# A fused cellular-automaton and convolution kernel: input rows asked for earlier, split rows of 256 columns, VectorE in program order

## The chip, the cores and the metric

The kernel runs on one core of a Trainium2 chip. A core has a matrix engine (TensorE, "PE"; its weight loads are "PEld"), a vector engine (VectorE, "DVE"), an activation engine (ScalarE, "ACT"), a general engine (GpSimd, "POOL") and a queue engine (SyncE, "SP") that here only issues DMAs. The engines run side by side and wait for each other through semaphores. Sixteen DMA engines carry all transfers. The metric is the time on the device in microseconds; lower is better.

## The reference

The input x has 32 images of 8 channels of 256 x 256 float32. Two layers follow each other, each on a group-normalised input. Layer 0, with the constants put in:

```python
drive = grid = x                       # x is normalised here, [32, 8, 256, 256]
for _ in range(15):                    # the lattice
    mapped = 3.9 * grid * (1.0 - grid)
    local = conv(mapped, K_local, groups=8)          # 3x3, each channel by itself
    physics = 0.7 * mapped + 0.3 * local
    grid = 0.85 * physics + 0.15 * drive
cml = clip(grid, 0.0001, 0.9999)
h = relu(conv(x, Wp, bp))              # NCA: 3x3, 8 -> 128 channels
nca = sigmoid(conv(h, Wu, bu))         # 1x1, 128 -> 8
gin = concatenate([x, cml, nca])       # 24 channels
g = sigmoid(conv(relu(conv(gin, Wg1, bg1)), Wg2, bg2))   # the gate: 3x3, then 1x1
out0 = g * cml + (1.0 - g) * nca
```

`out0` is added to the raw input. Layer 1 normalises the sum, quantises it to whole numbers between -127 and 127 with one scale for the whole batch, convolves it 3x3 from 8 to 8 channels, scales back, adds a bias and adds its own input.

## The kernel before

The program has two phases. Phase one computes layer 0, phase two layer 1. Phase two can start only when the largest value of all images is known.

Phase one works on eight groups of four images, and four kinds of work run in it at once:

- **Normalising** (`normalise`, L293 to L387). A pair of channels of one image is loaded into `xr`. VectorE takes statistics (L314, L315). TensorE averages them over the partitions (L322, L355) and VectorE finishes mean and deviation (L323 to L327, L357). GpSimd takes the power -1/2 of the variance (L358, `rstd_x`). VectorE then scales `xr` (L361). The result is written to memory twice. ScalarE copies it into `xq`, four column phases apart, for lattice and gate (`gs_s`). For NCA it is split in two float32 numbers of fewer digits, `hi` by a VectorE cast (L372) and `lo`, the rest, by a GpSimd subtraction (L373), which go to `xp_s` (L342). A row of `xp_s` has `PW` = 258 columns, of which the first and the last are zero, and so have the rows of the tiles `hi` and `lo`.
- **The lattice** (`lattice`, L392 to L557). One unit is one channel of four images, held in two sets `s` = 0, 1. A step of one set is a "half" (`half`, L480). Its matmuls (L499) fill two PSUM units `pt`. After each of three blocks of them a very small matmul `mark` follows (L274). VectorE empties the units into `gt` (L510) and computes the next state from `gt` (L520), each in two pieces. The state swaps between two layouts, `m_a` and `m_b`. After a half that writes `m_b`, GpSimd masks an edge (L525). After a half that writes `m_a`, SP issues two DMAs that exchange rows between tiles (`exchange`, L474 and L475), and the next step of this set needs them. 15 steps of two sets in 64 units are 1920 halves. The sources of the next unit (`d_a`, `d_b`, L462) and the stores of the last one also go out on SP, four after each half.
- **NCA** (`nca`, L576 to L644). An image is done in eight tiles of 32 rows. The input tile `im` of a tile has four DMAs (`rows`, L561 to L573). A unit (`hidden`, L579) is twelve matmuls (L585) into one PSUM unit, which ScalarE empties into `h` (L593). Eight units make a tile. After every two of them a drain of four matmuls (L601) follows, into `acc`. The tiles of `im` come from a pool with two buffers.
- **The gate** (`gate`, L705 to L836), one group behind. A tile has 120 matmuls (L759) over three sources `gin`, each of which takes two DMAs (`stage`, L656, L663). The same function also issues the two DMAs of `mix` (L672), which holds the values to be mixed. The rest of a tile is a list of "chores": mixing (`gate` and `y` on VectorE, L723 and L724), arranging (`f` on ScalarE, `d` and `f` on GpSimd, L685 to L689), staging the next tile, statistics (`st_y`, L730) and extremes with the store (`mx`, `mn`, L733 to L735).

These four are Python generators. `together` (L844) runs the lattice as the main one. After each half it takes one chore from the list, and then lets the others advance in proportion to fixed weights. The order in which the program states its instructions comes from this.

TensorE keeps this order as it stands. For the four other engines a scheduler decides the order, with the program's order as a priority:

```python
one.enter_context(tc.manual_schedule(engines={mybir.EngineType.PE}))
```

All PSUM units of lattice, NCA, gate and averages come from one pool `ps_u` with three buffers, so a unit can be written only when the one three places earlier has been emptied. All DMAs of phase one that the change touches are issued by SP, one after the other. An SP instruction that waits holds up those behind it.

NCA asks for the rows of the next tile after the sixth of the eight units, before the third drain:

```python
if i == 2:
    if done:
        nc.sync.dma_start(*done)
        done = None
    if t < NT8 - 1:
        ahead = rows(b, t + 1)
    elif all((b + 1, g) in ready for g in range(4)):
        loaded[b + 1] = rows(b + 1, 0)
```

Of the kernel before, what the change touches and what calls it, by code (L numbers as in the profile page):

```python
# [40 lines left out]
P = 128  # L41
# [11 lines left out]
PROWS = 268  # L53
ROW = 2 * C * PW
PART = PROWS * C * W
# [54 lines left out]
def kernel(  # L110
# [50 lines left out]

    xp_s = [dp.tile([PROWS, 2, C, PW], F32, name=f"xp_s{i}") for i in range(NBUF)]
    gs_s = [dp.tile([3, PROWS, C, W], F32, name=f"gs_s{i}") for i in range(NBUF)]
    y_s = [dp.tile([PROWS, C, W], F32, name=f"y_s{b}") for b in range(B)]

    with tc.tile_pool(name="prep", bufs=1) as pp, tc.tile_pool(name="prep2", bufs=2) as pp2:
# [23 lines left out]
        for t, at, n, w, rows in (  # L190
            *((t, 0, 2 * C, PW, ((0, 1), (257, 1))) for t in xp_s),
            *((t, j * PART, C, W, ((0, 1), (257, 1))) for t in gs_s for j in range(3)),
            *((t, 0, C, W, ((0, 1), (257, 5), (262, 5), (267, 1))) for t in y_s),
        ):
            k = 64 if w == W else 43
            for row, m in rows:
                borders.append(
                    (
                        dram_ap(t, at + row * n * w, [[w, m * n], [k, w // k], [1, k]]),
                        zt[: m * n, :k].unsqueeze(1).to_broadcast([m * n, w // k, k]),  # L200
                    )
                )
# [52 lines left out]
    with ExitStack() as one:  # L255


        one.enter_context(tc.manual_schedule(engines={mybir.EngineType.PE}))

# [3 lines left out]
        hp, xp, sp2, gp, gip = pool("hp", 4), pool("xp", 3), pool("sp2", 1), pool("gp", 3), pool("gip", 2)  # L263
        st, imp, wk, np_ = pool("st", 2), pool("imp", 2), pool("wk", 2), pool("np", 1)
        ps_u, ps_a, ps_m = pool("ps_u", 3, space=PSUM), pool("ps_a", 1, space=PSUM), pool("ps_m", 1, space=PSUM)
# [10 lines left out]
        fixed = lambda shape, name, dt=F32: np_.tile(shape, dt, name=name)  # L276
        hi, lo = fixed([P, 2, 2, PW], "hi", F32R), fixed([P, 2, 2, PW], "lo", F32R)
        for t in (hi, lo):
            for w in (0, PW - 1):
                G.memset(t[:, :, :, w].bitcast(F32), 0.0)  # L280
# [12 lines left out]
        def normalise(jobs):  # L293
# [36 lines left out]
            def stores(b, g, xq):  # L330
# [9 lines left out]
                for h in range(2):  # L340
                    for j, src in enumerate((hi, lo)):
                        nc.sync.dma_start(  # L342
                            dram_ap(
                                xp_s[b % NBUF],
                                (1 + P * h) * ROW + (C * j + 2 * g) * PW,
                                [[ROW, P], [PW, 2], [1, PW]],
                            ),
# [4 lines left out]
            def end(b, gs, xrs, e):  # L352
# [6 lines left out]
                for g, xr in zip(gs, xrs):  # L359
# [10 lines left out]
                    )  # L370
                    inner = lambda t: t[:, :, :, 1 : 1 + W]
                    V.tensor_copy(inner(hi), xr)  # L372
                    G.tensor_tensor(inner(lo), xr, inner(hi).bitcast(F32), ALU.subtract)  # L373
                    yield 0.05
# [186 lines left out]
        def rows(b, t):  # L561

            im = imp.tile([P, 2, 8, PW], F32R, name="im", tag="im")
            for k in range(2):
                for q in range(2):
                    nc.sync.dma_start(
                        im.bitcast(F32)[64 * q : 64 * q + 48, k],
                        dram_ap(
                            xp_s[b % NBUF], (32 * t + 16 * k + 8 * q) * ROW, [[PW, 48], [ROW, 8], [1, PW]]
                        ),  # L570
                    )
            return im
# [3 lines left out]
        def nca(b):  # L576
# [45 lines left out]
            for t in range(NT8):  # L622
                im = ahead
                acc = ps_a.tile([P, 512], F32, name="acc", tag="acc")
                for i in range(4):
                    hs = {}
                    for n in (i, i + 4):
                        hs[n], hs[n + 8] = hidden([im[64 * q : 64 * q + 48, :, n, :] for q in range(2)])
                        yield 1.4
                    if i == 2:  # L630
                        if done:
                            nc.sync.dma_start(*done)
                            done = None
                        if t < NT8 - 1:
                            ahead = rows(b, t + 1)
                        elif all((b + 1, g) in ready for g in range(4)):
                            loaded[b + 1] = rows(b + 1, 0)
                    if pend:
# [16 lines left out]

        def stage(b, t):  # L656

            src = gs_s[b % NBUF]
            gin = []
            for j in range(3):  # L660
                t_ = gip.tile([P, 4, W], F32, name=f"gin{j}", tag=f"gin{j}")
                for h in range(2):
# [5 lines left out]
                    )  # L668
                gin.append(t_)
            mix = gip.tile([P, 3, 2, W], F32, name="mix", tag="mix", bufs=1)  # L670
            for k in range(2):
# [3 lines left out]
                )  # L675
            return gin, mix

# [16 lines left out]
        def begin_gate(b):  # L694
            return scales(b), stage(b, 0)

# [8 lines left out]
        def gate(b):  # L705
# [39 lines left out]
            for t in range(NT8 + 1):  # L745
# [32 lines left out]

                def stage_(now):
                    if now["t"] < NT8 - 1:  # L780
                        now["ahead"] = stage(b, now["t"] + 1)
                    elif (b + 1) % GB:
                        staged[b + 1] = begin_gate(b + 1)

# [5 lines left out]

                steps = []
                if last:
                    steps.append(mix_)
                if t < NT8:
                    steps += [arrange_, stage_]
                if last:
# [280 lines left out]
```

## Time and profile before

Three runs took 13316.33 us in the median. The profile is of one execution.

| | |
|---|---|
| median of 3 runs (lowest to highest) | 13316.33 us (13310.97 to 13325.59) |
| profiled execution, its own time | 13288.75 us |
| profiled execution, span from first to last instruction | 13287.0 us |
| mean granted TensorE clock | 0.913 of full speed |
| DMA packets | 2486569, 1769.32 MB |
| DMA queue of SP | 58.7% of sixteen engines' span |
| start until NCA's first matmul | 206.6 us |
| phase one with lattice | until about 12340 us |
| last group's gate alone | until about 12720 us |
| phase two | the rest |

How to read it. A line of waits names the engine and the tile that waited, the one that ended the wait, the sum in microseconds, how often, and the longest. A wait with "issue" was ended by nothing that the profile shows. In a timeline a row gives start, duration, engine, line and operation, what is written from what, how many instructions were merged, and in brackets the idle time of the engine just before it. Each program matmul of four-byte numbers can stand as several records. PEclk is the clock that TensorE was granted; a digit of 9 means 0.9 to 1.0.

### The profile page before, as it was taken

Reading aid. Unit: us, or ns where it says so; the run is one execution under the profiler, and the core shown is the slowest. Engines: PE = TensorE matmul, PEld = TensorE weight load, DVE = VectorE, ACT = ScalarE, POOL = GpSimd, SP = SyncE. Lnnn points to the kernel's source line nnn. Section 1 sums busy time; section 2 is a strip of 40 time slices with the busy share of each in tenths; the row PEclk is TensorE's granted clock in tenths of the full one; section 3 lists DMA queues with packets and bytes.
Section 4 is the critical chain, followed back from the end, with each engine's and each line's share of the span. In section 5 each row is a group of like instructions: output and inputs, shape, how many; then the busy total and the mean of one; then the engine's idle time right before and its main releaser. Section 6 shows DMA issues by size and latency. Waiting matters only on the chain. (4 is left out here: it accounts for less than half of the span.)

```text
span 13287.0 us, 372338 instructions
## 1 busy us (share of the span) xinstructions
PE 11179.9 (84%) x165152; PEld 6938.4 (52%) x165152; DVE 7782.5 (59%) x11376; ACT 3789.6 (29%) x4034; POOL 1552.4 (12%) x2242
## 2 busy tenths in 40 slices
PE   4888888888888888888888888888888989889754
PEld 2555555555555555555555555555555555555532
DVE  4555555555555565555555556555655655556477
ACT  2222222222222222222222222222222222222233
POOL 1000011111111111111111111111111110001200
PEclk7999999999999999999999999999999999999877
DMA  6554566565666656665665666656666565555778
GB/s 164 94 102 95 102 134 129 123 132 127 135 127 130 134 128 126 130 136 122 132 132 123 134 135 130 127 127 132 128 132 133 127 127 116 113 109 123 179 242 257
DMA packets 2486569, 1769.32 MB, mean 133 GB/s; under 512 B 1034336, under 2 KB 2456032, under 8 KB 2484832
## 3 DMA queue, kind: packets, MB, share of 16 engines
q1 hardware_dynamic: 2392416, 1655.96, 58.7%
q10 hardware_dynamic: 92544, 89.54, 2.2%
q8 instruction: 1299, 21.28, 0.7%
q14 instruction: 310, 2.54, 0.1%
HBM read 1133.84 MB, written 474.94 MB: 121 GB/s over the span
## 5 line engine op out<-in xcount | busy, mean ns | idle before, releaser
L593 ACT ACTIVATE h<-pt,bp_sb 128x1024 f32<-128x1024 f32 x2048 | 2273.9, 1112 | 5982.6 <-PE pt L585 5978.3
L585 PE MATMUL pt<-im,wp_hi 48*128 48x512 f32 x12288 | 2869.3, 440 | 942.8 <-DMA im<-xp_s 769.3
L510 DVE SCALAR_TENSOR_TENSOR gt<-pt,d_b 128x650 f32<-128x650 f32 (+1 forms) x1920 | 1463.8, 763 | 2432.7 <-PE mark L274 1389.4
L499 PE MATMUL pt<-m_a,lw 64*64 64x325 f32 (+1 forms) x30720 | 2464.9, 439 | 354.9 <-DMA m_a<-m_a 223.6
L585 PE MATMUL pt<-im,wp_lo 48*128 48x512 f32 x12288 | 2660.7, 410 | 0.0
L510 DVE SCALAR_TENSOR_TENSOR gt<-pt,d_a 128x640 f32<-128x640 f32 (+1 forms) x1920 | 1446.8, 754 | 2013.6 <-PE mark L274 1059.9
L585 PEld LDWEIGHTS pt<-im,wp_hi 48*128 48x128 f32 x12288 | 1340.5, 194 | 2096.5 <-issue 1460.1
L499 PE MATMUL pt<-m_b,lw 64*64 64x256 f32 (+1 forms) x30720 | 2360.9, 425 | 67.6 <-DVE gt L510 38.1
L499 PEld LDWEIGHTS pt<-m_a,lw 64*64 64x64 f32 x30720 | 1462.2, 140 | 1185.8 <-issue 455.8
L499 PEld LDWEIGHTS pt<-m_b,lw 64*64 64x64 f32 x30720 | 1413.5, 136 | 881.8 <-issue 457.2
L759 PE MATMUL pt<-gin,gw 48*32 48x192 f32 (+2 forms) x61440 | 1321.0, 305 | 240.4 <-issue 228.7
L759 PEld LDWEIGHTS pt<-gin,gw 48*32 48x32 f32 x61440 | 1150.2, 109 | 588.8 <-issue 367.9
L585 PEld LDWEIGHTS pt<-im,wp_lo 48*128 48x128 f32 x12288 | 1345.7, 195 | 208.0
L520 DVE SCALAR_TENSOR_TENSOR m_a<-gt 128x640 f32<-128x640 f32 (+1 forms) x1792 | 1414.3, 789 | 58.5
L520 DVE SCALAR_TENSOR_TENSOR m_b<-gt 128x650 f32<-128x650 f32 (+1 forms) x1792 | 1385.7, 774 | 103.0 <-DVE gt L510 3.7
L525 POOL TENSOR_TENSOR m_b<-m_b,junk 128x36 f32<-128x36 f32 x896 | 241.9, 270 | 8498.1 <-DVE m_b L520 5232.4
L601 PE MATMUL acc<-h,wu_z 128*32 128x512 f32 x8192 | 1106.6, 611 | 0.0
L274 PE MATMUL mark<-qw 64*64 64x1 bf16 x5760 | 953.0, 165 | 3.2 <-issue 1.9
L687 POOL TENSOR_TENSOR d<-mix 128x256 f32<-128x256 f32 x512 | 554.7, 1101 | 1580.5 <-DVE gate L723 1146.5
L274 PEld LDWEIGHTS <-qw 64*64 64x64 bf16 x5760 | 642.8, 112 | 142.1 <-issue 10.3
L986 PE MATMUL pt<-qt,qw 128*128 128x512 bf16 (+1 forms) x864 | 235.0, 434 | 238.4 <-ACT ob L991 238.4
L685 ACT ACTIVATE f<-mix,sc 128x512 f32<-128x512 f32 x256 | 208.5, 815 | 679.5 <-DVE y L724 476.4
(109 smaller groups left out, 5445.8 us busy)
## 6 DMA issues: line engine op xcount, KB each, us to landing
im<-xp_s SPq DMA_DIRECT2D x1024, 387.0 KB
gin<-gs_s SPq DMA_DIRECT2D x1536, 192.0 KB
mix<-gs_s SPq DMA_DIRECT2D x512, 384.0 KB
d_a<-gs_s SPq DMA_DIRECT2D x2048, 36.0 KB
yb<-y_s ACTq DMA_DIRECT2D x28, 2432.0 KB
xp_s<-hi SPq DMA_DIRECT2D x256, 258.0 KB
xp_s<-lo SPq DMA_DIRECT2D x256, 258.0 KB
xr<-in_x_dram SPq DMA_DIRECT2D x128, 512.0 KB
```

The costliest lines, as they stand in the source:

```text
L274: T.matmul(one_[HIGH], qw[HIGH, 0, HIGH], qw[HIGH, 0, 0:1], start=True, stop=True)
L499: T.matmul(pt[dst], lw[src, c, w, dst], rhs[src], start=first, stop=not first)
L510: V.scalar_tensor_tensor(gt.rearrange("p (u c) -> p u c", u=2), pt[:, :, : w * n], FLOOR, d[:, ts, :].rearrange("p (u t) j -> p u (t j)", ...
L520: V.scalar_tensor_tensor(to, gt, 1.0, gt, ALU.subtract, ALU.mult)
L525: G.tensor_tensor(edge, edge, junk.unsqueeze(1).to_broadcast([P, TU, 2]), ALU.mult)
L585: T.matmul(ph[:, i, :].rearrange("p (h w) -> p h w", w=W), w[64 * i : 64 * i + 48, dx, :], rhs[:, :, dx : dx + W], start=(dx == 0 and w is ...
L593: S.activation(h.rearrange("p i c -> p (i c)"), ph.rearrange("p i c -> p (i c)"), AF.Relu, bias=bp_sb)
L601: T.matmul(acc[32 * g : 32 * g + 32], wu_z[:, 24 - 8 * i : 56 - 8 * i], hs[4 * g + i], start=(i == 0), stop=(i == 3),)
L685: S.activation(f, flat(mix[:, 0]), AF.Identity, bias=sc[:, 0:1], scale=sc[:, 2:3])
L687: G.tensor_tensor(d[:, cols], mix[:, 1, k], mix[:, 2, k], ALU.subtract)
L759: T.matmul(pa[32 * i : 32 * i + 32, h, to], gw[64 * h : 64 * h + 48, j, dx, :], gin[j][64 * h : 64 * h + 48, i, of], start=(j == 0 and n = ...
L986: T.matmul(pt[:, i:j, :], w[:, dx, :], qt[b % 2][h][:, k0 + i : k0 + j, dx : dx + W], start=(dx == 0), stop=(dx == 2),)
```

## The change

It has four parts.

1. NCA's `rows` of the next tile are issued after the first unit of a tile (`n == 0`), not after the sixth. The store of the tile before stays where it was.
2. `xp_s` has rows of 256 columns. `hi` and `lo` lose their two border columns. `im` is no longer taken from a pool: two fixed tiles `ims`, of which the border columns are zeroed once, take turns, and the DMAs write between the borders. A DMA's rows are now 1024 bytes where they were 1032.
3. `stage` is cut in two. `inputs` loads the three `gin` and becomes the first chore of a gate tile. `blend` loads `mix` and stays where `stage` was.
4. VectorE, too, keeps the program's order in phase one.

```diff
-ROW = 2 * C * PW
+ROW = 2 * C * W
...
-    xp_s = [dp.tile([PROWS, 2, C, PW], F32, name=f"xp_s{i}") for i in range(NBUF)]
+    xp_s = [dp.tile([PROWS, 2, C, W], F32, name=f"xp_s{i}") for i in range(NBUF)]
...
-            k = 64 if w == W else 43
+            k = 64
...
-        one.enter_context(tc.manual_schedule(engines={mybir.EngineType.PE}))
+        one.enter_context(tc.manual_schedule(engines={mybir.EngineType.PE, mybir.EngineType.DVE}))
...
-        hi, lo = fixed([P, 2, 2, PW], "hi", F32R), fixed([P, 2, 2, PW], "lo", F32R)
-        for t in (hi, lo):
+        hi, lo = fixed([P, 2, 2, W], "hi", F32R), fixed([P, 2, 2, W], "lo", F32R)
+        ims = [fixed([P, 2, 8, PW], f"im{i}", F32R) for i in range(2)]
+        for t in ims:
             for w in (0, PW - 1):
                 G.memset(t[:, :, :, w].bitcast(F32), 0.0)
...
-                                (1 + P * h) * ROW + (C * j + 2 * g) * PW,
-                                [[ROW, P], [PW, 2], [1, PW]],
+                                (1 + P * h) * ROW + (C * j + 2 * g) * W,
+                                [[ROW, P], [W, 2], [1, W]],
...
-                    inner = lambda t: t[:, :, :, 1 : 1 + W]
-                    V.tensor_copy(inner(hi), xr)
-                    G.tensor_tensor(inner(lo), xr, inner(hi).bitcast(F32), ALU.subtract)
+                    V.tensor_copy(hi, xr)
+                    G.tensor_tensor(lo, xr, hi.bitcast(F32), ALU.subtract)
...
-            im = imp.tile([P, 2, 8, PW], F32R, name="im", tag="im")
+            im = ims[(NT8 * b + t) % 2]
             for k in range(2):
                 for q in range(2):
                     nc.sync.dma_start(
-                        im.bitcast(F32)[64 * q : 64 * q + 48, k],
+                        im.bitcast(F32)[64 * q : 64 * q + 48, k, :, 1 : 1 + W],
                         dram_ap(
-                            xp_s[b % NBUF], (32 * t + 16 * k + 8 * q) * ROW, [[PW, 48], [ROW, 8], [1, PW]]
+                            xp_s[b % NBUF], (32 * t + 16 * k + 8 * q) * ROW, [[W, 48], [ROW, 8], [1, W]]
                         ),
...
                         hs[n], hs[n + 8] = hidden([im[64 * q : 64 * q + 48, :, n, :] for q in range(2)])
+                        if n == 0:
+                            if t < NT8 - 1:
+                                ahead = rows(b, t + 1)
+                            elif all((b + 1, g) in ready for g in range(4)):
+                                loaded[b + 1] = rows(b + 1, 0)
                         yield 1.4
-                    if i == 2:
-                        if done:
-                            nc.sync.dma_start(*done)
-                            done = None
-                        if t < NT8 - 1:
-                            ahead = rows(b, t + 1)
-                        elif all((b + 1, g) in ready for g in range(4)):
-                            loaded[b + 1] = rows(b + 1, 0)
+                    if i == 2 and done:
+                        nc.sync.dma_start(*done)
+                        done = None
...
-        def stage(b, t):
+        def inputs(b, t):
...
+            return gin
+
+        def blend(b, t):
+
+            src = gs_s[b % NBUF]
             mix = gip.tile([P, 3, 2, W], F32, name="mix", tag="mix", bufs=1)
...
-            return gin, mix
+            return mix
...
-                def stage_(now):
+                def inputs_(now):
                     if now["t"] < NT8 - 1:
-                        now["ahead"] = stage(b, now["t"] + 1)
+                        now["ahead"] = [inputs(b, now["t"] + 1)]
                     elif (b + 1) % GB:
-                        staged[b + 1] = begin_gate(b + 1)
+                        staged[b + 1] = [inputs(b + 1, 0)]
+
+                def blend_(now):
+                    if now["t"] < NT8 - 1:
+                        now["ahead"].append(blend(b, now["t"] + 1))
+                    elif (b + 1) % GB:
+                        staged[b + 1] = scales(b + 1), (*staged[b + 1], blend(b + 1, 0))
...
                 steps = []
+                if t < NT8:
+                    steps.append(inputs_)
                 if last:
                     steps.append(mix_)
                 if t < NT8:
-                    steps += [arrange_, stage_]
+                    steps += [arrange_, blend_]
...
-                while t < NT8 - 1 and "ahead" not in now and chores:
+                while t < NT8 - 1 and len(now.get("ahead", ())) < 2 and chores:
                     chores.pop(0)()
```

More of the change, by code (lines that the diff above doesn't have):

```diff
@@ L190 @@
         for t, at, n, w, rows in (
-            *((t, 0, 2 * C, PW, ((0, 1), (257, 1))) for t in xp_s),
+            *((t, 0, 2 * C, W, ((0, 1), (257, 1))) for t in xp_s),
             *((t, j * PART, C, W, ((0, 1), (257, 1))) for t in gs_s for j in range(3)),
@@ L263 @@
         hp, xp, sp2, gp, gip = pool("hp", 4), pool("xp", 3), pool("sp2", 1), pool("gp", 3), pool("gip", 2)
-        st, imp, wk, np_ = pool("st", 2), pool("imp", 2), pool("wk", 2), pool("np", 1)
+        st, wk, np_ = pool("st", 2), pool("wk", 2), pool("np", 1)
         ps_u, ps_a, ps_m = pool("ps_u", 3, space=PSUM), pool("ps_a", 1, space=PSUM), pool("ps_m", 1, space=PSUM)
@@ L694, in begin_gate @@
         def begin_gate(b):
-            return scales(b), stage(b, 0)
+            return scales(b), (inputs(b, 0), blend(b, 0))
         PARTS = (
```

## The prediction

> **What bounds the kernel now.** I read the page first, then the waits of TensorE and VectorE, the busy times by stage, and last the order of time around one wait.
>
> ```profile
> PE 11179.9 (84%) x165152; PEld 6938.4 (52%) x165152; DVE 7782.5 (59%) x11376; ACT 3789.6 (29%) x4034; POOL 1552.4 (12%) x2242
> ...
> PEclk7999999999999999999999999999999999999877
> DMA  6554566565666656665665666656666565555778
> ```
>
> TensorE is busiest, at less than full clock nearly throughout. The stage table (span, then busy PE, PEld, DVE, ACT, POOL, granted clock, DMA share, GB/s) shows where:
>
> ```profile
> 0.00:330.00 330.00, 142.22 (x1388) 90.32 (x1388) 157.60 (x341) 74.75 (x59) 51.53 (x72) 0.78 0.70 164
> ...
> 1000.00:12200.00 11200.00, 9785.84 (x145949) 6105.44 (x145950) 6553.73 (x9807) 3201.43 (x3330) 1329.64 (x1924) 0.93 0.61 126
> 12200.00:12740.00 540.00, 404.19 (x10551) 267.87 (x10547) 243.28 (x379) 116.92 (x146) 134.25 (x175) 0.84 0.73 182
> ```
>
> In the long stage PE idles 1414 of 11200 us, and a clock of 0.93 (the records know only 1 and 0.5) means half speed for a seventh of it. Its waits:
>
> ```profile
> PE pt L585 <- DMA im<-xp_s: 769.3, 166, 22.6
> PE pt L986 <- ACT ob L991: 238.4, 29, 12.3
> PE pt L759 <- issue: 228.7, 208, 4.4
> PE pt L499 <- DMA m_a<-m_a: 223.6, 81, 13.0
> PE pt L585 <- ACT h L593: 105.7, 88, 2.7
> ```
>
> The first is NCA waiting for its input rows. One such wait, TensorE's rows in order of time:
>
> ```profile
> 11943.01 1.07 PE L601 MATMUL acc<-h,wu_z 128*32 128x512 f32 x8
> 11952.26 0.76 PE L585 MATMUL pt<-im,wp_hi 48*128 48x512 f32 x1 [8.19 <-DMA im<-xp_s]
> 11955.05 0.79 PE L585 MATMUL pt<-im,wp_hi 48*128 48x512 f32 x1 [2.02 <-DMA im<-xp_s]
> ...
> 11957.90 1.79 PE L499 MATMUL pt<-m_a,lw 64*64 64x325 f32 x11
> ...
> 11961.96 0.50 PE L585 MATMUL pt<-im,wp_hi 48*128 48x512 f32 x2
> ```
>
> The loads were issued at 11940.8, PE ran dry at 11944. The lattice group that starts at 11957.90 takes 1.79 us; the same group takes 0.99 at 11940.70. So a wait is paid twice: idle, then some 6 us at half clock. Over 330 to 12200 us the trace has 744 us of idle ended by im. Of the clock records there, 189 stretches are at 0.5; for 89 of them the longest idle just before is an im wait, PE is busy 637 us within them, and full clock would have saved half, 318 us. Im's price is therefore 744 + 318 = 1062 us. Everything else that idles or slows PE in that stretch is 1505 - 744 = 761 idle and (1085 busy at half clock) / 2 - 318 = 225 lost.
>
> [...] rows of 1032 bytes, read from a 1032-byte pitch, take 105 ns a packet for im; packets of 1024 bytes average 58.9, and 46 at the median. [...]
>
> **The change part by part.** Durations are of the profiled execution, 13288.75 us (span 13287.0); the median of the runs, 13316.33, lies 27.6 above it, and I add that at the end.
>
> *Im asked for earlier.* The four loads of tile t+1 move from i == 2 to after the first unit of tile t: five NCA units (1.6 us each, 5004.84 to 5006.43) and two drains (1.0) sooner, plus the lattice and gate work between. I followed the built instruction order and its semaphores of both kernels, from each tile's last load back to the latest PE instruction on which its issue depends (through SP's queue too), and added PE's work from there to the first use at traced full-clock durations: unit 1.6, lattice half 2.3, gate tile 5.25, drain 1.0 us. Before: 10 to 11 us for a quarter of the 256 tiles, median 20.5. After: at least 33, median 43, but for the very first tile. In the trace a load's last packet is 3.3 to 11.4 us behind its issue (5th to 95th percentile), with 2.8 to 3.2 us to issue four; the longest wait was 22.6. 33 covers all that. I keep 5% for the first tile and collisions: -705 idle, -302 clock. The bounds are -600 and -1062 together.
>
> The loads go out of SP earlier, so what stands behind them counts: they can only start once PE has left the buffer of tile t-1, and in the new order no exchange (L474, L475) depends on a PE instruction more than 1 us of work past its own half, as before. So SP isn't held; the shared engines are, next.
>
> *Rows of 256 columns.* Packet counts stay (1024 x 384 for im, 512 x 256 for the stores). The stores' 1032-byte packets took 61 to 65 ns already and gain little. [...] their SBUF rows keep a 1032-byte pitch. The nearest row is 256-byte packets into d_b, also at an odd pitch (260 bytes), at about 20 ns against 18 for d_a's even rows, so I take 59 ns: 393216 x 46 / 16 = 1130 us less engine time, four loads in 5.7 instead of 10.1 us. Bounds: 46 and 105 ns. It is worth nothing directly on PE, but shortens what an exchange stands behind. The cast to hi (128 x 0.69) and lo (128 x 2.19) lose their gaps: 0, since neither is what PE waits for.
>
> *The exchange.* The long stage runs 1750 halves (28001 + 28000 records at 32 a half) in 11200 us, 6.4 each. One exchange chain is 2.3 PE, 3.1 DVE (0.83 + 0.84 + 0.69 + 0.70), 1.3 SP, 1.7 to the last packet[...]: 8.9 of two halves' 12.8, slack 3.9. At 5.8 us a half the slack is 2.7. All waits of 10 us and over on m_a in the trace have im just ahead in SP's queue; these shrink. But where im and PE used to be late together, an exchange issued behind four loads now lands some 4 us late by itself, 1.3 past its slack: for about half of 256 loads that is 170 us. Against 277 now (219 idle + 58 clock) I take 377, +100; bounds -150 and +400.
>
> *Program order on VectorE.* Before, the scheduler put gate's five operations (0.69 + 1.19 + 0.70 + 0.67 + 0.68 = 3.9 us) in one block, and drained a half as gt, m, gt, m. Now it is gt, gt, m, m, so the second PSUM unit is free 0.84 us sooner, and gate's work is spread: gate and y after one half, st_y after another, mx and mn after a third. By the same count, all 256 gate multiplications stood within 3 us of the PE work they wait for; now 67 do.
>
> ```profile
> DVE gate L723 <- ACT gate L717: 280.7, 102, 13.3
> DVE stats L314 <- DMA xr<-in_x_dram: 219.2, 66, 15.7
> DVE xr L361 <- POOL rstd_x L358: 78.0, 116, 5.0
> ```
>
> What it adds: xr now directly follows rstd_x, so VectorE stands for GpSimd's power (0.73, and behind d or lo 2.2 more) with lattice's gt queued behind. At most 128 x 1.7 = 220 against 78 now; DVE is idle 41% of the time, so PE sees perhaps a fifth. PE's waits ended by gt are 116 idle + 44 clock, those by rstd_x 40 + 14. I take -75; bounds -160 and +110.
>
> *Gate's sources first.* Gin's loads come before mix's. By the same count, gin's lowest quarter rises from 26 to 31 us of PE work, median 39 either way. PE waits for gin 11.2 us in all. In 12200 to 12740 the queues keep nearly the same order: 0, bounds -15 and +15.
>
> *Start and phase two.* Start is bound by xr and stores (DMA 0.84 to 0.96): 0, -15 to +30. Phase two is unchanged.
>
> Sum: -705 - 302 + 100 - 75 = -982; 13288.75 - 982 = 12307, with the 27.6 on it 12334.
>
> **The rivals.**
> - *Giveback.* The chains behind im (exchange, ACT h, gt) were also late, and half of im's price comes back in them: -1062 / 2, so 12785. For: m_a waits of up to 13 us exist already. Against: their slack is above 2.5 us[...].
> - *All waits shrink.* Im's packets fall to 46 ns, exchange -150, VectorE -160, im -1062: 13316 - 1372 = 11944. For: all four push the same way. Against: a faster PE uses up every slack.
> - *The exchange takes over, slower.* If im's packets stay at 105 ns and all 256 loads stand ahead of an exchange, it lands 8 us late, 5.3 past 2.7 of slack, plus about 1 us of clock: 256 x 6.3 = 1613 against 1007 gained: 13920. It decides from 3.9 us a load. Against: loads stood ahead of exchanges before, and m_a waited 224 us in all.
> - *The move does nothing*, since the scheduler orders SP: excluded by the order's count, but for a DMA rate below 50 GB/s.
>
> **How the numbers follow.** Forecast 0.74 (its own range 12130 to 12560), giveback 0.14, all shrink 0.08, exchange slower 0.03, nothing 0.01. The range reaches into both neighbours: 12080 to 12700. About 0.2% (27 us) is what can be told from no change: faster 0.96, same 0.01, slower 0.03.
>
> **What would show it.** Right: PE's wait for im under 60 us; a clock of 0.95 or more in the long stage; im's packets near 59 ns and a DMA share there near 0.57; m_a's wait 200 to 400; gate's wait on ACT below 150. Wrong: an m_a or gt wait above 600, or im's wait above 200 with the loads out early, which would mean the engines, not the issue, were late.

## The result and the profile after

The changed kernel took 13115.76 us in the median of 4 runs (13107.69 to 13129.27), beside 13313.65 us for the kernel before (4 runs, 13306.98 to 13325.59). The ratio is 0.9849, with a 95% interval of 0.9833 to 0.9864. The profiled execution took 13112.92 us, with a span of 13111.1. The change gained 1.5%; the prediction had 7.4%.

The busy times, the clock and the DMA share in 40 slices, and the DMA queue that carries instructions, from the page:

```profile
PE 11150.6 (85%) x165152; PEld 6918.5 (53%) x165152; DVE 7547.9 (58%) x11376; ACT 3760.1 (29%) x4034; POOL 1633.7 (12%) x2242
...
PEclk8999999999999999999999999999999999999777
DMA  6544556656666665665666566556665655555788
...
q8 instruction: 1299, 21.28, 0.8%
```

The long stage in the table by stage (span, then busy PE, PEld, DVE, ACT, POOL, granted clock, DMA share, GB/s):

```profile
1000.00:12200.00 11200.00, 9899.64 (x148450) 6170.94 (x148446) 6429.59 (x9938) 3213.49 (x3372) 1429.77 (x1956) 0.94 0.60 127
```

PE did 1.7% more matmul records in this stretch (148450 against 145949), but its clock rose only from 0.93 to 0.94 and the DMA share is about what it was (0.60 after 0.61). What PE waited for:

```profile
PE pt L764 <- issue: 709.4, 256, 8.5
PE pt L499 <- DMA m_a<-m_a: 304.0, 103, 12.5
PE pt L999 <- ACT ob L1004: 243.6, 28, 12.8
PE pt L585 <- ACT h L593: 192.4, 132, 3.0
...
PE pt L585 <- DMA im<-xp_s: 17.9, 2, 16.3
```

The wait that the change was priced by is gone: im 769.3 to 17.9 us. But the gate's matmuls (L764, L759 before) now stand 709.4 us on "issue", against 228.7, with the longest 8.5 us against 4.4. "Issue" means that the profile shows nothing that PE waited for.

What idle time did to the clock, counted in the trace after between 330 and 12200 us. The clock records have 1 and 0.5 only, and each lasts a whole number of steps of 3.41 us. Of PE's idle times that began at full clock, 140 of 141 of 3 us and over were followed by a record of 0.5 that began at most 4 us after their end, and so were 98 of 292 between 1 and 3 us and 8 of 280 between 0.1 and 1 us. A drain of four matmuls (L601) took 1.93 us within records of 0.5 and 1.07 at full clock (medians of 14 and 958). The half-clock loss below is an estimate from these records, half of PE's busy time within those of 0.5; at full clock the drain was 0.86 of its 1.93 us shorter.

The largest entries of the balance, with that loss between 330 and about 12000 us put to the longest idle just before each stretch, as the prediction did:

| what ended PE's wait | idle, us | lost at half clock, us | together |
|---|---|---|---|
| im | 769 to 18 | 318 to 0 | -1069 |
| issue (idle: in the gate; half clock: anywhere) | 229 to 709 | 59 to 336 | +758 |
| m_a | 224 to 304 | 58 to 91 | +113 |
| h (idle: in NCA; half clock: anywhere) | 106 to 192 | 47 to 84 | +124 |
| gt | 103 to 57 | 44 to 24 | -66 |
| rstd_x | 41 to 23 | 14 to about 0 | -32 |

The sum of these rows is -172 us, and the spans differ by 175.9. The rows are not the whole account: smaller entries are left out (`PE pt L499 <- issue` rose by 47 us, others fell), and they nearly cancel. On this account 897 of the 1069 us that im gave up came back, 758 of them by waits with "issue", and 737 of these 758 in the gate.

### The profile page after: what moved, and what is told of

It is laid out like the page before. It is cut to its first block, busy times and chain, and to the rows that moved or that the text cites. A ratio compares the mean times of both kernels' runs of the same rounds, so it can differ in the third digit from the quotient of the medians.

```text
span 13111.1 us, 374007 instructions
## 1 busy us (share of the span) xinstructions
PE 11150.6 (85%) x165152; PEld 6918.5 (53%) x165152; DVE 7547.9 (58%) x11376; ACT 3760.1 (29%) x4034; POOL 1633.7 (12%) x2242
## 3 DMA queue, kind: packets, MB, share of 16 engines
q8 instruction: 1299, 21.28, 0.8%
## 4 chain that ended last, share of the span: by engine, by line
PE 67%; DMA 10%; issue 9%; DVE 7%; ACT 2%; SPq 2%; POOL 1%; ACTq 1%; POOLq 0%; DVEq 0%
PE pt L499 29%; PE pt L585 19%; PE pt L764 10%; PE acc L601 6%; DMA m_a<-m_a 4%; DMA yb<-y_s 3%; PE pt L720 2%; DVE gt L510 2%; ACT h L593 1%; DMA im<-xp_s 1%; DVE m_b L520 1%; ACTq L1010 1%; DVE m_a L520 1%; SPq L462 1%; DVE xr L362 1%
## 5 line engine op out<-in xcount | busy, mean ns | idle before, releaser
L585 PE MATMUL pt<-im,wp_hi 48*128 48x512 f32 x12288 | 2637.9, 425 | 227.7 <-ACT h L593 192.4
L499 PE MATMUL pt<-m_a,lw 64*64 64x325 f32 (+1 forms) x30720 | 2465.5, 439 | 394.8 <-DMA m_a<-m_a 304.0
L510 DVE SCALAR_TENSOR_TENSOR gt<-pt,d_a 128x640 f32<-128x640 f32 (+1 forms) x1920 | 1366.2, 752 | 2435.2 <-PE mark L274 1739.2
L499 PE MATMUL pt<-m_b,lw 64*64 64x320 f32 (+1 forms) x30720 | 2413.5, 433 | 120.6 <-DVE gt L510 44.7
L585 PE MATMUL pt<-im,wp_lo 48*128 48x512 f32 x12288 | 2452.6, 395 | 1.3 <-issue 1.3
L499 PEld LDWEIGHTS pt<-m_a,lw 64*64 64x64 f32 x30720 | 1479.3, 140 | 1235.2 <-issue 530.7
L764 PE MATMUL pt<-gin,gw 48*32 48x192 f32 (+2 forms) x61440 | 1445.6, 324 | 721.7 <-issue 709.4
L499 PEld LDWEIGHTS pt<-m_b,lw 64*64 64x64 f32 x30720 | 1445.8, 139 | 965.4 <-issue 505.5
L585 PEld LDWEIGHTS pt<-im,wp_hi 48*128 48x128 f32 x12288 | 1166.9, 186 | 1343.8 <-issue 719.4
L764 PEld LDWEIGHTS pt<-gin,gw 48*32 48x32 f32 x61440 | 1233.0, 115 | 1109.8 <-issue 876.1
L585 PEld LDWEIGHTS pt<-im,wp_lo 48*128 48x128 f32 x12288 | 1172.8, 187 | 206.1 <-issue 1.7
L601 PE MATMUL acc<-h,wu_z 128*32 128x512 f32 x8192 | 1119.9, 617 | 0.8 <-issue 0.8
L772 ACT ACTIVATE r<-pt,bv 128x512 f32<-128x512 f32 x256 | 175.9, 687 | 1809.6 <-PE pt L764 1809.6
L694 POOL TENSOR_TENSOR f<-f,mix 128x256 f32<-128x256 f32 x512 | 445.2, 889 | 28.3 <-ACT f L690 27.9
```

The costliest lines, as they stand in the source:

```text
L499: T.matmul(pt[dst], lw[src, c, w, dst], rhs[src], start=first, stop=not first)
L510: V.scalar_tensor_tensor(gt.rearrange("p (u c) -> p u c", u=2), pt[:, :, : w * n], FLOOR, d[:, ts, :].rearrange("p (u t) j -> p u (t j)", ...
L585: T.matmul(ph[:, i, :].rearrange("p (h w) -> p h w", w=W), w[64 * i : 64 * i + 48, dx, :], rhs[:, :, dx : dx + W], start=(dx == 0 and w is ...
L601: T.matmul(acc[32 * g : 32 * g + 32], wu_z[:, 24 - 8 * i : 56 - 8 * i], hs[4 * g + i], start=(i == 0), stop=(i == 3),)
L694: G.tensor_tensor(f[:, cols], f[:, cols], mix[:, 2, k], ALU.add)
L764: T.matmul(pa[32 * i : 32 * i + 32, h, to], gw[64 * h : 64 * h + 48, j, dx, :], gin[j][64 * h : 64 * h + 48, i, of], start=(j == 0 and n = ...
```

## Where the gate stops: PE's own instructions come late

One of these waits in order of time. TensorE's rows:

```profile
4862.36 1.07 PE L720 MATMUL pt<-r,gw 128*32 128x512 f32 x8
4863.36 2.63 PE L764 MATMUL pt<-gin,gw 48*32 48x256 f32 x127
4872.68 3.75 PE L764 MATMUL pt<-gin,gw 48*32 48x63 f32 x113 [6.68 <-issue]
4876.36 0.99 PE L499 MATMUL pt<-m_b,lw 64*64 64x320 f32 x11
```

And SP's queue around it:

```profile
4856.67 2.61 SPq L566 DMA_DIRECT2D im<-xp_s  x4
4859.33 1.90 SPq L462 DMA_DIRECT2D d_a<-gs_s  x4
...
4865.43 0.62 SPq L474 DMA_DIRECT2D m_a<-m_a  x1
```

The gate tile starts, and stops in the middle of its 240 matmuls for 6.68 us. The matmul behind the stop waits for no semaphore, and gin's loads for this tile had gone out at 4818.41, 45 us earlier. Four im loads went out from 6.7 us before its start on. The DMA queues of the core (packets, MB, share of 16 engines; the times of all packets are added, and from 4866 to 4870 us a median of 20 were under way at once, so a share can pass 100%), first from 4866 to 4870 us, then from 4870 to 4872:

```profile
q1 hardware_dynamic: 1084, 0.60, 120.3%
```

```profile
q1 hardware_dynamic: 456, 0.33, 57.7%
q8 instruction: 1, 0.02, 4.1%
```

For four microseconds of the wait the engines carry SP's transfers alone. With packets put to their loads in the order of issue, those of the four im loads run from 4858.93 to 4869.51 us. Then a single instruction packet comes, from 4870.07 to 4871.37, and PE goes on at 4872.68. What this packet carries can be told by counting, in the trace after if no other is named; a block here is 256 of PE's records in a row:

- All 1299 packets of q8 have 16384 bytes. PE's matmuls and weight loads (330304) and the records of its sequencer (2227) make 1298.95 blocks of 256. So q8 carries PE's instructions, one packet a block.
- Counted in all these records, the first matmul behind each of the gate's stops of over 0.4 us that "issue" ended stands at the same place of a block, give or take one record: 239 of 239, and 168 of 168 in the trace before.
- Between two such stops there are exactly as many instruction packets as blocks, in 238 of 238 cases, and PE goes on 1.4 us after a packet's end (median; 1.2 to 1.7 in 90% of the stops).
- A block's packet starts 1.1 us (median) after PE has entered the block before it: it comes one block ahead and no more. Where PE enters that block while packets of im run, the median is 4.8 us (251 blocks), elsewhere 0.9 us (1046 blocks).
- Of the gate's 709.4 us, 559 lie in the 134 stops that begin within 12 us of im's last load, 4.2 us each. The 122 others take 1.2 us each.

This also says why the gate is the place. A gate tile is 480 records in 5.25 us, so a block lasts 256 / 480 x 5.25 = 2.8 us there, while on average PE enters one every 13111 / 1299 = 10.1 us. A block needs 1.0 to 1.1 us until its packet starts (medians of the traces before and after), 1.2 for the packet, and 1.4 from its end to the next matmul: about 3.7. So the block that follows one lying wholly inside a gate tile is about 0.9 us late by this estimate from medians, even without a burst (e4 below measured 0.89 without im's loads). In 480 records there are 480 - 256 = 224 places at which such a block can begin, and every 256th record begins one, so of 256 tiles about 224 should have such a stop; that is what the 208 waits of before mostly were. The longest stop, of 8.5 us, began 3.9 us after im's last load was issued.

Before, the loads followed the sixth unit; after, the first. In the order of PE's records, with the prediction's durations, a gate tile comes within 12 us of PE's work behind the first unit in 55% of the tiles, behind the fourth in 19% and behind the sixth in 5%. (The expectation of e3 has 62% and 22%, counted in the built program.) NCA and gate both have eight tiles an image, so the two keep this distance. In the trace before, only 24 of the 208 stops begin within 12 us of im's last load.

## The experiments

Six theories are named by letters in the expectations. **F**: instruction blocks wait behind im's loads. **G**: the gate's sources first, or VectorE's order, starves the gate. **C**: the lattice's chain sets the pace and idle time is only renamed. **D**: VectorE's program order makes ACT stand, and so NCA's `h`. **A**: the place of im's rows in the on-chip memory (an odd pitch, a start at column 1) keeps its packets slow. **H**: im's loads are slow because one load writes 48 partitions of one half only. Ratios are to the kernel before, run beside each group on the same chip: it took 13318.15 us beside the experiments e, 13326.04 beside f and 13287.37 beside g. The kernel after was not run again beside them, so it is compared by its own ratio, 0.9849. Edits are to the kernel after unless another is named.

### Which part makes the stop

**e1_rows_late**, the first part undone:

```diff
-                        if n == 0:
-                            ...
-                    if i == 2 and done:
+                    if i == 2:
...
+                        if t < NT8 - 1:
+                            ahead = rows(b, t + 1)
```

> The changed kernel with NCA's loads asked for after the sixth unit again; its other three parts stay. Theory F (fetch): the changed kernel's stall of 709 us inside the gate's matmuls (ended by nothing the profile shows, 256 times) is PE waiting for its next block of instructions, whose DMA stands behind im's four loads. Then with the loads late the gate's stall falls back to about 230 us and im's wait returns to 600 to 800: about 13200 to 13350 us. Theory G (gin first or VectorE's order starves the gate): the gate keeps 600 us or more, im's wait is added, about 14000. Theory C (PE's pace is set by the lattice's chain, and the idle time only changes its name): about 13100, with the sum of PE's idle time as in the changed kernel.

13368.66 us, 1.0039 (1.0026 to 1.0052). Its waits of PE:

```profile
PE pt L585 <- DMA im<-xp_s: 748.3, 173, 15.9
PE pt L764 <- issue: 276.4, 212, 6.6
```

Both waits are back near what they were before, though gin is still first and VectorE still in program order. That speaks for F and against G. Parts two to four without the first are a little slower than the kernel before, and than F's range.

**e2_dve_free**, the fourth part undone:

```diff
-        one.enter_context(tc.manual_schedule(engines={mybir.EngineType.PE, mybir.EngineType.DVE}))
+        one.enter_context(tc.manual_schedule(engines={mybir.EngineType.PE}))
```

> The changed kernel with VectorE's order left to the scheduler again. F: the gate's stall stays at 650 to 750 us; VectorE's order is worth some 75 us by itself, so 13150 to 13250. G, if it is VectorE's order that starves the gate: the stall falls below 400 and the time to 12700. C: 13100 to 13130.

13040.07 us, 0.9792 (0.9775 to 0.9808). Its waits of PE:

```profile
PE pt L764 <- issue: 717.9, 268, 8.9
...
PE pt L585 <- ACT h L593: 103.0, 83, 3.2
PE pt L499 <- DVE gt L510: 89.5, 80, 5.8
```

The stop stays, as F said, and doesn't depend on VectorE's order. The time lies below F's range, because undoing the order gains where a loss was expected: the order costs 0.57% (0.9849 less 0.9792, 76 us). It takes 45 us of gt's wait away and adds 89 to that for `h`. D holds: with the order, the ACT instruction just ahead of a late `h` is `f`, which stands for VectorE's `y`, in 60 cases (65.5 us of the waits for `h`), and a scaling of `d_a` or `d_b` in 27 (46.3 us). With VectorE free these are 8 (3.7 us) and 18 (15.9 us). The two differences, 62 and 30 us, are all of the 89, since the rest went down by 3.

**e3_rows_mid**, the loads after the fourth unit (the units run as n = 0, 4, 1, 5, ...):

```diff
-                        if n == 0:
+                        if n == 5:
```

> The changed kernel with the loads after the fourth unit (n == 5), where by the instruction order only 22% of them have a gate tile within the next 12 us of PE work (62% after the first unit), with 19 us of PE work left until their first use. F: the gate's stall falls to 250 to 400 us, im's wait stays below 150: 12600 to 12800. G: stall as before, 13100 to 13250. C: 13100.

12676.09 us, 0.9513 (0.9492 to 0.9534). Im's wait is 20.6 us, and the gate's:

```profile
PE pt L764 <- issue: 343.3, 206, 8.9
```

The same loads in the same burst, only at another distance from the gate tile: three times the gain. Time and stop lie in F's ranges and outside those of G and C.

**e4_no_rows**, the loads of the first two tiles only (1016 of 1024 left out, so NCA works on old rows):

```diff
-            for k in range(2):
+            for k in range(2 if NT8 * b + t < 2 else 0):
```

> The changed kernel without im's loads after the first two tiles: NCA computes every other tile on old rows, all its matmuls stay; 1016 of 1024 loads (398 MB) are left out. F: the gate's stall falls below 200 us, im's wait is nil, exchange waits below 100: 12100 to 12300. G: the stall stays above 600, above 12800. C: little changes, 13000 to 13100.

12031.62 us, 0.9038 (0.9025 to 0.9052). Its waits of PE:

```profile
PE pt L585 <- ACT h L593: 233.6, 144, 3.9
...
PE pt L764 <- issue: 180.6, 203, 3.5
PE pt L499 <- DMA m_a<-m_a: 114.1, 54, 7.7
```

Without the transfers the 203 stops take 180.6 / 203 = 0.89 us each, the 0.9 of the sum above. The clock from 1000 to 11000 us is 0.98. C falls: 1084 us go with im's transfers (13115.76 less 12031.62), and the lattice follows; that is even less time than F's range, though the exchange waits of 114 us miss its "below 100". What this run can't tell is whether the stops shrink for want of im's burst or of DMA load in general (the share there falls to 0.41).

### Where im's packets lose their time, and whether gains add

**f1_mid_free**, e3 and e2 together:

```diff
-        one.enter_context(tc.manual_schedule(engines={mybir.EngineType.PE, mybir.EngineType.DVE}))
+        one.enter_context(tc.manual_schedule(engines={mybir.EngineType.PE}))
...
-                        if n == 0:
+                        if n == 5:
```

> Loads after the fourth unit and VectorE left to the scheduler: both single edits in one kernel. Theory F (PE's instruction fetch behind im's loads) and D (VectorE's program order makes ScalarE stand for f and d_a in front of h) act at different places, so the gains add: 12676 - 76 = 12600 us, PE's wait for h back to about 105. If they are the same slack counted twice: 12660 or more.

12650.41 us, 0.9490 (0.9473 to 0.9508). The interval meets that of e3: freeing VectorE is worth 0.23% here, not 0.57%, so the two gains don't simply add. The wait for `h` falls from 176.3 to 86.7 us, but m_a's rises from 329.0 to 385.1 and gt's from 32.1 to 60.3.

**f2_aligned**, im's rows at a pitch of 288 columns and with data from column 16:

```diff
-        ims = [fixed([P, 2, 8, PW], f"im{i}", F32R) for i in range(2)]
+        ims = [fixed([P, 2, 8, 288], f"im{i}", F32R) for i in range(2)]
...
-            for w in (0, PW - 1):
+            for w in (15, 272):
...
-                        im.bitcast(F32)[64 * q : 64 * q + 48, k, :, 1 : 1 + W],
+                        im.bitcast(F32)[64 * q : 64 * q + 48, k, :, 16 : 16 + W],
...
-                        hs[n], hs[n + 8] = hidden([im[64 * q : 64 * q + 48, :, n, :] for q in range(2)])
+                        hs[n], hs[n + 8] = hidden([im[64 * q : 64 * q + 48, :, n, 15 : 15 + PW] for q in range(2)])
```

> The changed kernel with im's rows in SBUF on a pitch of 1152 bytes, data from byte 64 on, instead of 1032 and 4. Im's packets took 105 ns before and 109 after, so the rows' place in memory was not their cost. Theory A (their place in SBUF): packets fall to 55 to 75 ns, the gate's stall to about 350 us, 12650 to 12800. Theory H (48 partitions of one half[...]): packets stay above 95 ns, time 13050 to 13130.

13026.05 us, 0.9774 (0.9759 to 0.9788). Im's packets take 104.3 ns on average against 108.6 after, nowhere near the 59 of the prediction: A falls. The kernel is still 0.75% of the time before faster than the one after; 34 us less on issue is a part, the rest is not explained.

**f3_spread**, one of the four loads after each of the first four units:

```diff
-        def rows(b, t):
+        def rows(b, t, ks=(0, 1, 2, 3)):
...
                 for q in range(2):
+                    if 2 * k + q not in ks:
+                        continue
...
-                        if n == 0:
+                        piece = {0: 0, 4: 1, 1: 2, 5: 3}.get(n)
+                        if piece is not None:
                             if t < NT8 - 1:
-                                ahead = rows(b, t + 1)
+                                ahead = rows(b, t + 1, (piece,))
...
```

> The changed kernel with one of im's four loads after each of the units 1, 2, 3 and 4, instead of all four after unit 1. F: never more than one load (2.6 us of the engines) stands ahead of PE's instructions, so the gate's stall falls to 250 to 400 us; the last load has 19 us left, im's wait below 100; exchanges stand behind shorter bursts, below 250: 12500 to 12700. If it is the amount of data and not its burst: stall about 700, 13050 to 13150.

12432.51 us, 0.9323 (0.9309 to 0.9337), faster than F's range, with a stop of the gate just above the range named for it:

```profile
PE pt L769 <- issue: 404.0, 223, 7.1
PE pt L499 <- DMA m_a<-m_a: 139.4, 94, 4.5
```

Im's packets take 96.9 ns. As many bytes, asked for from the same unit on, without the burst: 5.3% of the time before faster than after.

**f4_halves**, all at once after the first unit as in the kernel after, but as eight loads of four rows. The two halves of the partitions took turns before, too, load by load; now they do so in smaller pieces:

```diff
-            for k in range(2):
+            for k, r in ((0, 0), (0, 4), (1, 0), (1, 4)):
                 for q in range(2):
                     nc.sync.dma_start(
-                        im.bitcast(F32)[64 * q : 64 * q + 48, k, :, 1 : 1 + W],
+                        im.bitcast(F32)[64 * q : 64 * q + 48, k, r : r + 4, 1 : 1 + W],
...
-                            xp_s[b % NBUF], (32 * t + 16 * k + 8 * q) * ROW, [[W, 48], [ROW, 8], [1, W]]
+                            xp_s[b % NBUF], (32 * t + 16 * k + 8 * q + r) * ROW, [[W, 48], [ROW, 4], [1, W]]
```

> The changed kernel with eight loads of four rows instead of four of eight, the two partition halves in turn, as gin's loads are (70 ns a packet). H: the two halves overlap more, packets fall to about 75 ns, the gate's stall to about 400: 12750 to 12850. A: packets stay at 105 to 110, and SP issues twice as many: 13100 to 13150.

12545.53 us, 0.9413 (0.9399 to 0.9427). Im's packets take 90.0 ns, the gate waits 422.8 us on issue. The time beats what H expected, while the packets fall short of it. So H fits in part, but isn't shown: 108.6 to 90.0 ns agrees in direction, but these loads are also smaller and there are twice as many, and f3 lowers the packet to 96.9 ns with its loads as they were, so no run here shows what taking turns between the halves does alone.

### Both together, and the parts by themselves

**g1_pairs**, f3 and f4 together, a pair of half loads after each of the first four units:

```diff
-        def rows(b, t):
+        def rows(b, t, pieces=((0, 0), (0, 4), (1, 0), (1, 4))):
...
-            for k in range(2):
+            for k, r in pieces:
...
-                        if n == 0:
+                        piece = {0: (0, 0), 4: (0, 4), 1: (1, 0), 5: (1, 4)}.get(n)
+                        if piece:
                             if t < NT8 - 1:
-                                ahead = rows(b, t + 1)
+                                ahead = rows(b, t + 1, (piece,))
...
```

> The changed kernel with im's loads cut into eight of four rows, a pair (one of each partition half) after each of the units 1 to 4: the spreading (12433) and the halves in turn (12546) at once. F and H: bursts of 2.2 us at packets of 85 to 90 ns; the gate's stall 300 to 400 us, exchange waits about 130: 12340 to 12430. If the two share one effect: 12430 to 12480.

12097.22 us, 0.9103 (0.9087 to 0.9119), more than expected. Its waits of PE, and its stretch from 1000 to 11000 us in the columns of the table by stage:

```profile
PE pt L767 <- issue: 262.3, 213, 3.8
PE pt L1002 <- ACT ob L1007: 234.2, 28, 10.4
PE pt L585 <- ACT h L593: 194.2, 132, 3.0
...
PE pt L499 <- DMA m_a<-m_a: 89.0, 68, 4.0
```

```profile
1000.00:11000.00 10000.00, 9354.04 (x144736) 5830.81 (x144732) 6262.01 (x9692) 3135.95 (x3293) 1395.90 (x1905) 0.98 0.60 140
```

All 1024 x 384 packets of im are carried, at the DMA share of after (0.60), and 140 GB/s. Yet the longest stop of the gate is 3.8 us, m_a's longest wait 4.0, the clock 0.98, and im's packets take 79.4 ns. Where PE enters a block while packets of im run, the packet of the next one starts 1.1 us later (median), beside 4.8 in the trace after, 2.4 in f4 and 1.7 in f3. This is what e4 couldn't tell: the burst is the cause of most of the stop, not the load on the engines. Of the 709.4 us, 447 go without it (262.3 are left), and 82 more when the transfers go, too (180.6 in e4).

**g2_pairs_free**, g1 with VectorE free as in e2:

```diff
-        one.enter_context(tc.manual_schedule(engines={mybir.EngineType.PE, mybir.EngineType.DVE}))
+        one.enter_context(tc.manual_schedule(engines={mybir.EngineType.PE}))
```

> The same with VectorE left to the scheduler. D: PE's wait for h falls by some 90 us, exchange waits rise a little: 30 to 75 us below the kernel with pairs alone. If VectorE's order only mattered where the gate stalled: no difference.

12068.56 us, 0.9086 (0.9064 to 0.9109), the best median of the kernels that carry all loads, not told apart from g1. The wait for `h` falls to 106.6 us, while gt's is 62.5 (35.1 in g1) and m_a's 118.8.

**g3_no_gin**, the third part undone, with gin and mix loaded in one chore again:

```diff
                 steps = []
-                if t < NT8:
-                    steps.append(inputs_)
...
-                    steps += [arrange_, blend_]
+                    steps += [arrange_, stage_]
```

> The changed kernel with gin's and mix's loads in one chore again, after arranging; the three other parts stay. F: gin's loads are not what starves the gate, stall 650 to 750, time within 60 us of 13116. G (gin's loads asked for first stand in front of PE's instructions): stall below 450, under 12850.

13142.85 us, 0.9892 (0.9871 to 0.9913). The gate's wait on issue is 762.9 us, as long as with the part, and e2 showed the same for VectorE's order: G falls. Gin first is worth 0.43% (0.9892 less 0.9849; the two intervals just don't meet), of which the prediction had nothing.

**g4_only_move**, the kernel before with the first part alone:

```diff
+                        if n == 0:
+                            ...
                         yield 1.4
-                    if i == 2:
-                        ...
+                    if i == 2 and done:
+                        nc.sync.dma_start(*done)
+                        done = None
```

> The kernel before with im's loads after the first unit, and nothing else. F: the move alone turns im's wait (769 us) into the gate's stall (650 to 750 us), 13000 to 13080, as the changed kernel with VectorE freed (13040); rows of 256 columns and gin first are worth nothing. If the rows of 256 columns carry the gain: 13250 to 13320.

13125.26 us, 0.9877 (0.9861 to 0.9894). Its waits of PE:

```profile
PE pt L759 <- issue: 731.5, 248, 8.1
PE pt L499 <- DMA m_a<-m_a: 302.0, 96, 12.9
```

The move by itself, with rows of 258 columns, a free VectorE and gin beside mix, makes the whole stop. The time lies above F's range of 13000 to 13080, and F was wrong that the other parts are worth nothing: parts two and three together are worth 0.85% (0.9877 less 0.9792 of e2), and part four takes 0.57% back. Rows of 256 columns were not run alone. On im's packets they did nothing: at the late place 103.6 ns (e1) beside 105.0 (before), at the early place 108.6 (after) beside 107.5 (g4).

## Why the prediction missed

The sign was right (0.96 for faster), the size was not: 12334 predicted with a range from 12080 to 12700, and 13116 measured. That the sign held is partly luck: 897 of the 1069 us came back at places that the prediction had not priced or had priced lower, and nothing in its sum kept that share below the whole. By its own steps:

- **Im asked for earlier: right by itself.** -705 and -302 were predicted, -751 and -318 came. The order count held: PE stands for im twice in the whole run.
- **The step that failed is the sum of the move: it had no term for what stands behind im's loads other than the exchange.** The prediction said that "the shared engines are, next", and then priced only SP's own queue on them. PE's instruction blocks, on q8, stand behind im's loads as well (0.9 us to a packet's start, 4.8 within a burst). Both hints were in the lines it read: the page lists q8 with 1299 packets and 21.28 MB, and the quoted wait "PE pt L759 <- issue: 228.7, 208, 4.4" is an engine idle in the midst of a tile's matmuls with nothing visible to wait for. The missing term is +481 idle and +277 at half clock, 758 of the 806 us between the predicted -982 and the -176 of the spans; 737 of the 758 fall in the gate.
- **Rows of 256 columns: wrong on im.** 59 ns a packet was taken from packets of other transfers; 108.6 were measured, against 107.5 with rows of 258 columns at the same place (g4). So a source pitch of 1024 bytes in place of 1032 brought im's packets nothing here, while the rows of the tile kept their pitch of 1032; packets of other transfers were no measure of it. The stores, which were taken to gain little, went from 61 and 65 ns to 50 and 51. The upper bound of 105 had been named, but the forecast took the nearer row. f4 and g1 reached 90.0 and 79.4 ns by other means.
- **The exchange: right in size.** +100 was taken; +80 idle and +33 at half clock came. It came at packets of 108.6 ns, not of the 59 that the step assumed, so the agreement is in part chance. The chain of 8.9 us in that step holds 0.5 us for semaphores that was the author's estimate and that no trace showed; its other four parts add up to 8.4.
- **Program order on VectorE: wrong sign.** -75 was taken, +76 measured by e2, inside the bounds of -160 and +110. The step looked at VectorE's operations and at what follows `rstd_x`; there it was right (that wait grew from 78.0 to 137.4 us and PE hardly saw it). It did not ask which ACT instruction then stands for VectorE ahead of `h` (`f` and the scalings, 92 us by e2).
- **Gate's sources first: too small.** 0 was taken, with bounds of 15; g3 gives about 55 us of gain (0.43% of 13116).

VectorE's waits after, in which the gate's multiplication was to fall below 150 us:

```profile
DVE gate L728 <- ACT gate L722: 258.5, 52, 12.0
DVE xr L362 <- POOL rstd_x L359: 137.4, 128, 3.5
```

Half as many waits as before (102), but hardly less time. Of the signs named for being right, gate "below 150", the clock of 0.95 (0.94), the packets of 59 ns and the DMA share of 0.57 (0.60) failed, while im below 60 and m_a between 200 and 400 held. Of the signs of being wrong none came: the time went to a place for which none had been named.

Of the rivals, "giveback" had the right shape, a wait that takes the place of the one removed, but at the wrong places: m_a, h and gt together took 171 us (113 + 124 - 66). One premise of "the exchange takes over" came true (packets above 105 ns) and its outcome did not: the exchange's slack was enough, the instruction block's was not.

Open remain the 0.75% of f2, how much rows of 256 columns bring alone, and why a block's single packet is late. In the example above four microseconds of q1 alone went by before it. But it does not always wait for the whole burst: in 74% of the 251 cases it starts before the last of im's packets has ended. When a block is asked for, the profile doesn't show, so no run here tells which part of the request is late.

## What to carry to other kernels

Count the instructions of the densest stretch of TensorE: here a block of 256 lasted less there than the time from entering a block to having the next (2.8 against 3.7 us), so TensorE's own instructions were a transfer with no slack. Its mark was a wait ended by "issue" within a run of matmuls, at the same place of a block of 256 each time. When a transfer is moved earlier, price everything that will stand behind it on the sixteen engines, instruction blocks included, and look at what code comes next, not only at what the transfer feeds. A burst that was split into shorter loads and spread over several units cost less than a tenth of what it cost as a whole: against the kernel without these loads (ratio 0.9038), the same bytes cost 8.1% of the time before in one piece (0.9849) and 0.65% in pairs (0.9103).

## What the runs showed of the hardware that was not expected

- The packet with TensorE's next 256 instructions started only 1.0 to 1.1 us (medians before and after) after TensorE had entered the block before, and TensorE went on 1.4 us after the packet's end. In code of 91 instructions per us (480 / 5.25) that is a stop of 0.89 us on average even without im's loads (e4_no_rows).
- Within a burst of another queue the same packet started later: 4.8 us in bursts of 10.4 us (medians, trace after), 1.1 us where the same bytes came in short pieces (g1).
- In a burst of four, a load of 48 partitions by 8 rows of 1024 or 1032 bytes took 104 to 109 ns a packet: 105.0 read and written at a pitch of 1032 bytes (before), 108.6 read at 1024 and written at 1032 (after), 104.3 read at 1024 and written at 1152 (f2). The same loads one after each unit took 97 ns, loads of half the rows 90 ns, and pairs of these apart in time 79 ns.
